# A post-norm decoder layer: cross attention's output kept as two halves, the routing arithmetic cut into single steps, and VectorE and TensorE held to the written order

## The chip, the cores and the metric

The kernel runs on one core of a Trainium2 chip. A core has a matrix engine (TensorE, PE in the profile, with its weight loads as PEld), a vector engine (VectorE, DVE), a scalar engine for activations (ScalarE, ACT), a general engine (GpSimd, POOL) and a synchronising engine (SyncE, SP) that mostly issues transfers. Each takes its instructions in order; they wait for each other by semaphores, and 16 DMA engines move data between the on-chip memory (SBUF), the accumulators (PSUM) and DRAM. The metric is the device time of one execution in microseconds, as the median of several runs. Everything is computed in fp32 precision.

## What is computed

The reference is one decoder layer on x of 16 batches of 100 tokens, 512 wide (1600 tokens), cut here to what matters:

```python
x = layernorm(x + self_attention(x))               # 16 heads of 32
x = layernorm(x + cross_attention(x, ctx))         # 16 query heads of 128, 4 key heads, 361 keys
x = layernorm(x + moe(x))                          # 8 experts, the best 2 for each token

def cross_attention(hidden, enc, mask):
    q = rmsnorm(hidden @ Wq + bq);  k = rmsnorm(enc @ Wk + bk);  v = enc @ Wv + bv
    probs = softmax(q @ k.T / sqrt(128) + mask)    # 4 query heads share a key head
    return (probs @ v) @ Wo

def moe(x):
    logits = x @ router_w + router_b
    vals, idx = top_k(logits, 2);  w = softmax(vals)
    h = silu(x @ expert_w[e] + expert_b[e])        # for the two experts of each token
    out = (sum of w * h) @ proj_w + proj_b
    y = x + out
    return norm_w * y / sqrt(mean(y * y) + 1e-6)
```

## The kernel before

**Pairs.** A product in fp32 precision is made of three products of rounded operands. `split` (L134) turns a tensor into a `Pair`: the high half is a copy rounded to fp32r (L139 on ScalarE, or L141 on VectorE), and the low half is what the rounding left, a subtraction (L142, on VectorE or GpSimd). `mm3` (L145) then issues high by high, high by low and low by high (L147 to L149), and `mmk` does so over the pieces of the contraction. So every operand of a product costs two element-wise passes ahead of it.

**Stages.** (a) Self attention by groups of four batches. (b) Its output product, the first layernorm, and the queries of cross attention, which are stored to DRAM (`qd`). (c) Cross attention, a loop over 64 steps (batch b, key head g), each with four heads. A step loads and splits its queries (`x_load`), makes scores (`x_scores`), exponentials and their scaling, transposes the probabilities and splits them (`x_turn`), and multiplies with the values (`x_attend`). When the third piece of keys is done, `x_attend` copies the accumulator `av` to a tile `o` on ScalarE (L839), adding the bias of the values, and stores it to `od` in DRAM (L844); there are two such tiles. During the same steps the keys and values of the next batch are projected. (d) The output product of cross attention: 13 tiles t of up to 128 tokens, each in four *parts* (t, g). `d_load` (L869) loads a part of `od`, splits it (high on ScalarE, low on GpSimd and VectorE in turn), `d_part` (L878) multiplies it: 12 products of 512 columns with 3 for each of the four heads, so 12 `mm3` products in all. `d_norm` (L898) adds the residual and does the second layernorm on VectorE, with two short activations on ScalarE in between; `d_turn` (L980) transposes the result, and `d_logits` (L997) makes the router's logits. The last three tiles (TAIL) are taken together, g outermost. (e) The experts: the tokens are sorted into 32 slots of 128 rows, each of one expert. `e_gather` fetches the rows of a slot by an indirect transfer from GpSimd's queue, `e_turn` transposes and splits them, `e_product` multiplies with the expert's weights, which are addressed by a register, and `e_out` adds the bias and applies Silu. (f) Gathering the two results of each token, the last product, and the two last norms.

**Routing.** `choose` (L1110) finds the two best experts of three tiles at a time, and each token's rank within its expert; `settle` (L1204) works out which slots are open, and `slots` (L1306) turns that into row indices by 36 or more tiny products. All of it is small VectorE arithmetic, 0.15 to 1.5 us each, in one long chain of dependences with a few products in it. It is done twice: for the first nine tiles, which give the first 11 slots, and for the rest.

**Order.** The program is written as a sequence, but the scheduler of the tile framework (`schedule_with_timeline_sim=True`) decides the order on each engine from its own model of durations; a dependence of the kind "no semaphore, order only" (`in_turn`, `tc.keep_in_program_order`) ties two instructions of an engine, and `tc.high_priority` moves a group ahead. In the kernel before, the routing functions are issued in one go at their place in the text, with high priority for the second round, and the weights of an expert are loaded by `load_expert` (L1389), four rows in one go. The parts that the scheduler put into the end of cross attention are products that fill PE's time between the dependent steps there.

Of the kernel before, what the change touches and what calls it, by code (L numbers as in the profile page):

```python
# [19 lines left out]
KC = D // 128  # L20
# [43 lines left out]
def tile_decoder_layer(  # L64
# [69 lines left out]

    def split(dst, src, high=None, low=None):

        high, low = high or nc.scalar, low or nc.vector
        if high is nc.scalar:
            ins = nc.scalar.copy(dst.h, src)  # L139
        else:  # L140
            ins = high.tensor_copy(dst.h, src)  # L141
        low.tensor_tensor(dst.l, src, dst.h.bitcast(FP), ALU.subtract)  # L142
        return ins
# [77 lines left out]
    od = [dram.tile([128, NH, 128], FP, name=f"od_{t}") for t in range(NT)]  # L221
# [601 lines left out]
    def x_attend(b, g, i):  # L823
# [14 lines left out]
        o = w2.tile([128, GR, S], FP, name=f"o2_{b}_{g}", tag="o")  # L838
        nc.scalar.activation(o, av, AF.Identity, bias=bvT[:, g : g + 1])  # L839
        a = 0  # L840
        while a < S:
            t, r = divmod(b * S + a, 128)
            m = min(S - a, 128 - r)
            nc.sync.dma_start(  # L844
                od[t][:, g * GR : (g + 1) * GR, r : r + m], o[:, :, a : a + m]
            )
            a += m
# [13 lines left out]
    def d_open():  # L861
        kv_l.close()
        inp["d"] = pool(d_i, "d_in", 2)
# [5 lines left out]
    def d_load(i):  # L869
        t, g = parts[i]  # L870
        n = TT[t][1]
        p = inp["d"]
        of = p.tile([128, GR, 128], FP, name=f"of_{t}_{g}", tag="of")
        nc.sync.dma_start(of[:, :, :n], od[t][:, g * GR : (g + 1) * GR, :n])
        OT[t, g] = pair(p, [128, GR, 128], f"ot_{t}_{g}", tag="ot")
        split(OT[t, g][:, :, :n], of[:, :, :n], low=nc.vector if i % 2 else nc.gpsimd)
# [20 lines left out]

    def d_norm(t):  # L898
        t0, n = TT[t]
        acc = X1.pop(t)  # L900
        p = w3 if t >= HEAD else inp["d"]
        x2 = p.tile([128, D], FP, name=f"x1_{t}", tag="x1", bufs=1 if t < HEAD else 3)
        nc.sync.dma_start(x2[:n], x1d[t][:n])
# [3 lines left out]
        X2[t] = x2  # L907
# [6 lines left out]
    for i, (b, g) in enumerate(order):  # L914
        if b == B - 1:
            if g == 0:
                d_open()
                d_load(0)
            for j in range(HEAD * g, HEAD * (g + 1)):
                d_load(j + 1)  # L920
                d_part(j)
                if parts[j][1] == NKV - 1:
# [36 lines left out]
    xsp = pool(fin, "k_x", 4, side="right")  # L959
    gs = ExitStack()  # L960
# [19 lines left out]
    def d_turn(t):  # L980
# [12 lines left out]
        nc.gpsimd.tensor_tensor(x2[:n], x2[:n], pb[:n], ALU.add)  # L993
# [115 lines left out]

    def choose(a, b):  # L1110
# [5 lines left out]
        for j in range(2):  # L1116

            nc.vector.tensor_reduce(top[:, j, a:b], vals, AX.X, ALU.max)
            hit = table("hit", sh)
            nc.vector.tensor_tensor(  # L1120
                hit, vals, top[:, j, a:b].unsqueeze(2).to_broadcast(sh), ALU.is_equal
            )
            nc.vector.tensor_tensor(hit, hit, num_b, ALU.mult)
            nc.vector.tensor_reduce(place[:, j, a:b], hit, AX.X, ALU.min)
            nc.vector.tensor_tensor(
# [4 lines left out]
            )  # L1130
            if j == 0:
# [3 lines left out]
                )  # L1135
                vals = rest
        if b == NT:

            nc.vector.memset(one[64:, :, NT - 1, :], 0.0)
        nc.vector.tensor_tensor(  # L1140
            chosen[:, a:b, :], one[:, 0, a:b, :], one[:, 1, a:b, :], ALU.add
        )
        for t in range(a, b):
            nc.vector.tensor_tensor(
                cum[:, t + 1, :], cum[:, t, :], chosen[:, t, :], ALU.add
            )
        o1, o2 = 2 * NE, (2 + m) * NE
# [21 lines left out]
        )  # L1169
        sh2 = [128, 2, m, NE]  # L1170
# [6 lines left out]
        )  # L1177
        rj = gw.tile([128, 2, m], FP, name=f"rj_{a}", tag=f"rj_{m}")
        nc.vector.tensor_reduce(rj, mine, AX.X, ALU.add)
        ri = gw.tile([128, 2, m], I32, name=f"ri_{a}", tag=f"ri_{m}")  # L1180
        nc.vector.tensor_copy(ri, rj)
        nc.vector.tensor_scalar(ri, ri, 127, None, ALU.bitwise_and)
        nc.vector.tensor_copy(lo[:, :, a:b], ri)

        nc.vector.tensor_scalar(rj, place[:, :, a:b], float(NE), None, ALU.add)
        nc.vector.scalar_tensor_tensor(
            opens[:, :, a:b], lo[:, :, a:b], 0.0, rj, ALU.is_equal, ALU.mult
        )
        if b == NT:
            nc.vector.memset(opens[64:, :, NT - 1 :], 0.0)  # L1190
            nc.vector.memset(token[64:, NT - 1 :], 0.0)

        for j in range(2):
            for t in range(a, b):
# [7 lines left out]
                )  # L1202

    def settle(a, b):  # L1204
# [5 lines left out]
        if a == 0:  # L1210
            by_128(full, count[:, m, :], "full")

        up = table("up", [128, m + 1, NE])
        nc.vector.tensor_scalar(up, count, 127.0, None, ALU.add)
        had = table("had", [128, m + 1, NE])
        by_128(had, up, f"had_{a}")

        opn = table("opn", sh)
        nc.vector.tensor_tensor(opn, had[:, 1:, :], had[:, :m, :], ALU.subtract)
        had = had[:, :m, :]  # L1220
        sh4 = [128, m, NE, NE]

        def before_it(these, here, less, name):
# [7 lines left out]
            )  # L1231
            new = table(name, sh)
            nc.vector.tensor_reduce(new, part, AX.X, ALU.add)
            nc.vector.tensor_reduce(here[:, a:b], these, AX.X, ALU.add)
            tri = parts_of([128, 1, m, b])[:, 0]
# [5 lines left out]
            )  # L1241
            till = table("till", [128, m])
            nc.vector.tensor_reduce(till, tri, AX.X, ALU.add)
            nc.vector.scalar_tensor_tensor(
# [6 lines left out]
            )  # L1251
            return new


        new = before_it(opn, opened, 0 if a else -EARLY, "new")
        if a == 0:
# [3 lines left out]
            )  # L1260
            nc.vector.tensor_tensor(fills, fills, opn, ALU.mult)
            first = before_it(fills, filled, 0, "first")
# [3 lines left out]
            )  # L1266

            nc.vector.scalar_tensor_tensor(
                fills, first, float(EARLY), fills, ALU.is_lt, ALU.mult
            )  # L1270
# [614 lines left out]
```

## Time and profile before

| | |
|---|---|
| median of 3 runs | 1400.51 us (1400.23 to 1403.87) |
| profiled execution, its own time | 1408.13 us |
| its span, first to last instruction | 1406.4 us |
| PE busy | 1331.6 us (95%) |
| VectorE busy | 942.8 us (67%) |
| ScalarE busy | 756.4 us (54%) |
| GpSimd busy | 710.3 us (51%) |
| mean granted clock of PE | 0.976 |

How to read it: the profile is one execution, 7.6 us longer than the median of the three timed runs, and 1.7 us of its time lie outside the span. A matmul's end is modelled, so a busy PE may hold slow products; the distance from one product's start to the next tells its pace. The stages lie about so: self attention to 200 us, stage (b) to 400, cross attention to 1074 with its first output parts from 993 on, the rest of the parts to about 1206, the experts to about 1365, the end to 1406.

### The profile page before, as it was taken

What the parts mean: (1) busy time and instruction counts of PE and PEld (TensorE: products, weight loads), DVE (VectorE), ACT (ScalarE), POOL (GpSimd) and SP (SyncE); (2) the same over time, 40 slices, a digit from 0 to 9 for tenths busy, and PEclk for the clock granted to TensorE, in tenths of its full rate; (3) what the DMA queues carried; (4) which work ended last, traced back from release to release, by engine and by line L of the source; (5) the groups of instructions that cost most, each with busy time, mean ns of one, the idle gap of its engine ahead of it and who ended that gap; (6) DMA issues with size and microseconds to landing.
All of it is one profiled execution on the core that took longest, in us unless ns stands there. A gap on an engine that the chain in (4) does not pass through costs nothing.

```text
span 1406.4 us, 25135 instructions
## 1 busy us (share of the span) xinstructions
PE 1331.6 (95%) x7928; PEld 1105.0 (79%) x7928; DVE 942.8 (67%) x2933; ACT 756.4 (54%) x1897; POOL 710.3 (51%) x840
## 2 busy tenths in 40 slices
PE   8999989999999999999999999999999898899894
PEld 7888868888778888888888888878887676677773
DVE  5776677776467777777777767767654558754576
ACT  4666643444446666666666666656654233333356
POOL 6878753344245555555555555545455444532530
PEclk9999989999999999999999999999999999899997
DMA  5221363544442122322233312322446545667883
GB/s 170 68 74 58 124 194 96 131 92 114 100 94 72 42 70 71 76 78 70 71 76 78 74 46 67 73 68 51 118 101 182 178 167 164 211 214 240 256 252 118
DMA packets 199160, 161.74 MB, mean 115 GB/s; under 512 B 133581, under 2 KB 153265, under 8 KB 199029
## 3 DMA queue, kind: packets, MB, share of 16 engines
q1 hardware_dynamic: 189191, 139.77, 36.2%
q0 software_dynamic: 4576, 14.95, 3.4%
q10 hardware_dynamic: 5262, 5.41, 1.3%
q8 instruction: 65, 1.06, 0.3%
q14 instruction: 66, 0.54, 0.1%
HBM read 107.25 MB, written 50.99 MB: 113 GB/s over the span
## 4 chain that ended last, share of the span: by engine, by line
PE 68%; DVE 14%; DMA 7%; ACT 4%; issue 3%; POOL 1%; SPq 1%; ACTq 1%; DVEq 0%; POOLq 0%
PE pq L147 4%; PE pq L148 4%; PE pq L149 4%; PE pv L147 4%; PE pv L148 4%; PE pv L149 4%; PE ptp L819 3%; PE pk L147 3%; PE pk L149 3%; PE pk L148 3%; PE s L147 3%; PE s L148 3%; PE s L149 3%; PE av L148 2%; PE av L147 2%
## 5 line engine op out<-in xcount | busy, mean ns | idle before, releaser
L811 POOL TENSOR_SCALAR p<-p,sums 100x361 f32<-100x361 f32 x256 | 146.4, 577 | 99.4 <-DVE sums L810 88.2
L798 DVE CUSTOM_DVE_ANT_0 p<-s,nmask 100x361 f32<-100x361 f32 x256 | 133.0, 527 | 63.4 <-PE s L149 54.7
L809 ACT ACTIVATE p<-p,nm 100x361 f32<-100x361 f32 x256 | 153.2, 601 | 39.6 <-DVE nm L798 36.3
L142 DVE TENSOR_TENSOR pT_l<-ptp,pT_h 128x400 fp32r<-128x400 f32 (+1 forms) x192 | 107.5, 568 | 57.2 <-ACT pT_h L139 56.8
L147 PE MATMUL pq<-WH 128*128 128x512 f32 (+2 forms) x272 | 107.2, 394 | 5.3 <-DVE WH L141 5.3
L819 PE MATMUL ptp<-ident,p 100*128 100x100 f32 (+1 forms) x768 | 107.4, 252 | 0.0
L139 ACT CAST pT_h<-ptp 128x400 fp32r<-128x400 f32 (+1 forms) x192 | 91.2, 487 | 30.1 <-PE ptp L819 29.7
L142 POOL TENSOR_TENSOR cT_l<-cf,cT_h 128x512 fp32r<-128x512 f32 (+1 forms) x48 | 54.4, 1133 | 103.4 <-ACT cT_h L139 101.5
L819 PEld LDWEIGHTS ptp<-ident,p 100*128 100x128 f32 (+1 forms) x768 | 95.4, 151 | 13.3 <-POOL p L811 2.3
L148 PE MATMUL pq<-WL,WH 128*128 128x512 f32 (+2 forms) x272 | 104.9, 385 | 0.0
L149 PE MATMUL pq<-WH,WL 128*128 128x512 f32 (+2 forms) x272 | 104.6, 385 | 0.0
L149 PE MATMUL acc<-WH,ot_l 128*128 128x512 f32 (+1 forms) x208 | 85.7, 413 | 7.3 <-DVE ot_l L142 5.8
L147 PE MATMUL acc<-WH,ot_h 128*128 128x512 f32 (+1 forms) x208 | 85.1, 409 | 5.0 <-ACT ot_h L139 5.0
L147 PE MATMUL s<-kT_h,WH 128*100 128x362 f32 x256 | 88.1, 355 | 0.7 <-ACT kT_h L139 0.7
L147 PE MATMUL av<-pT_h,WH 128*128 128x400 f32 (+1 forms) x192 | 76.8, 400 | 9.0 <-ACT pT_h L139 8.6
L666 POOL TENSOR_TENSOR qs<-qs,r_q 128x512 f32<-128x512 f32 (+1 forms) x52 | 54.0, 1068 | 60.9 <-DVE r_q L171 49.4
L149 PE MATMUL s<-kT_h,WL 128*100 128x362 f32 x256 | 84.3, 329 | 0.0
L148 PE MATMUL s<-kT_l,WH 128*100 128x362 f32 x256 | 83.7, 327 | 0.0
L148 PE MATMUL acc<-WL,ot_h 128*128 128x512 f32 (+1 forms) x208 | 83.6, 402 | 0.0
L142 POOL TENSOR_TENSOR WL<-qf,WH 128x400 fp32r<-128x400 f32 x64 | 67.3, 1052 | 30.5 <-ACT WH L139 26.9
L147 PE MATMUL pv<-WH,cT_h 128*128 128x512 f32 (+1 forms) x192 | 79.8, 416 | 0.9 <-DVE WL L142 0.9
L148 PE MATMUL pv<-WL,cT_h 128*128 128x512 f32 (+1 forms) x192 | 77.9, 406 | 0.0
(348 smaller groups left out, 3990.6 us busy)
## 6 DMA issues: line engine op xcount, KB each, us to landing
qf<-qd SPq DMA_DIRECT2D x64, 200.0 KB
of<-od SPq DMA_DIRECT2D x48, 256.0 KB
cf<-in_ctxT SPq DMA_DIRECT2D x16, 722.0 KB
eb<-in_expert_b SPq DMA_DIRECT2D x32, 256.0 KB
ysd<-h SPq DMA_DIRECT2D x32, 256.0 KB
f_e<-in_expert_w SPq DMA_DIRECT2D x30, 256.0 KB
f_wq<-in_Wq SPq DMA_DIRECT2D x16, 256.0 KB
f_wo<-in_Wo SPq DMA_DIRECT2D x16, 256.0 KB
```

The lines of the kernel that those rows point to most:

```text
L139: ins = nc.scalar.copy(dst.h, src)
L142: low.tensor_tensor(dst.l, src, dst.h.bitcast(FP), ALU.subtract)
L147: nc.tensor.matmul(out, a.h, b.h, start=start, stop=False)
L148: nc.tensor.matmul(out, a.h, b.l, start=False, stop=False)
L149: nc.tensor.matmul(out, a.l, b.h, start=False, stop=stop)
L666: nc.gpsimd.tensor_tensor(qr[:, hs, :], qr[:, hs, :], rs[:n, hs].unsqueeze(2).to_broadcast([n, GR, HD2]), ALU.mult,)
L798: nc.vector.tensor_tensor_reduce(out=p, in0=sc[:, :SE], in1=nmask, scale=1.0, scalar=BIG, op0=ALU.add, op1=ALU.min, accum_out=nm,)
L809: nc.scalar.activation(p, p, AF.Exp, bias=nm, scale=-1.0, accum_out=sh)
L811: nc.gpsimd.tensor_scalar(p, p, sh, 1.0, ALU.mult, ALU.mult)
L819: nc.tensor.transpose(pt[:n, h, :], probs[h][:, c0 : c0 + n], ident[:S, :S])
```

## The change

- *Halves in DRAM.* `od` holds, for each head, a high and a low half. At the end of a step `x_attend` makes the high half on ScalarE, as before but rounded, and the low half by one more VectorE instruction that reads `av` from PSUM, adds the bias and subtracts the high half. The tile `o` is twice as large, and there is one of it instead of two. Stores and loads of `od` carry twice the bytes, and `d_load` with its two splits is replaced by `d_fetch`, a transfer alone, which runs three parts ahead with four buffers.
- *Single steps.* `choose`, `settle` and `slots` are generators that yield after each VectorE instruction, and PAUSE ahead of the products that use what came before. `route(n)` issues the next n steps: 12 after each part, and 15, 14 and 11 between the expert products.
- *Program order.* `pin` ties all VectorE instructions, and all PE instructions, from part 12 (t = 3, g = 0) to the expert product in whose step the routing ends, each to the one before it in the text. ScalarE, GpSimd and SyncE are still ordered by the scheduler. With this the text itself is put in order: `d_turn(t - 1)` goes ahead of part g = 2 instead of g = 1, expert rows are split one at a time at given parts (`e_rows`), the residual is loaded ahead at g = 2 (`d_x1`), the first two slots are transposed ahead of the last two parts, the second round's products come after expert products 3 and 7 (counted from 0), gathers of slots are issued earlier, and the bias of the last three tiles (`d_bias`) after expert weights.
- *Gates.* The weights of the two experts were made by Exp, an addition, a reciprocal and a product; they are made by Tanh of half the difference of the logits and two affine instructions.

The diff, cut to its core:

```diff
-    od = [dram.tile([128, NH, 128], FP, name=f"od_{t}") for t in range(NT)]
+    od = [dram.tile([128, NH, 2, 128], FP, name=f"od_{t}") for t in range(NT)]
...
-        o = w2.tile([128, GR, S], FP, name=f"o2_{b}_{g}", tag="o")
-        nc.scalar.activation(o, av, AF.Identity, bias=bvT[:, g : g + 1])
+        o = w2.tile([128, GR, 2, S], FR, name=f"o2_{b}_{g}", tag="o", bufs=1)
+        bias = bvT[:, g : g + 1]
+        nc.scalar.activation(o[:, :, 0, :], av, AF.Identity, bias=bias)
+        nc.vector.scalar_tensor_tensor(
+            o[:, :, 1, :], av, bias, o[:, :, 0, :].bitcast(FP), ALU.add, ALU.subtract,
+        )
...
-    def d_load(i):
-        of = p.tile([128, GR, 128], FP, name=f"of_{t}_{g}", tag="of")
-        nc.sync.dma_start(of[:, :, :n], od[t][:, g * GR : (g + 1) * GR, :n])
-        OT[t, g] = pair(p, [128, GR, 128], f"ot_{t}_{g}", tag="ot")
-        split(OT[t, g][:, :, :n], of[:, :, :n], low=nc.vector if i % 2 else nc.gpsimd)
+    def d_fetch(upto):
+        for i in range(fetched[0], min(upto, len(parts))):
+            p = inp["d2" if i > HEAD * NKV and i % 4 == 2 else "d"]
+            o = p.tile([128, GR, 2, 128], FR, name=f"ot_{t}_{g}", tag="ot")
+            nc.sync.dma_start(o[:, :, :, :n].bitcast(FP), od[t][:, g * GR : (g + 1) * GR, :, :n])
+            OT[t, g] = Pair(o[:, :, 0, :], o[:, :, 1, :])
...
+    def route(n):
+        while n and routing:
+            what = next(routing[0], None)
+            if what is None and routing[0].gi_frame is None:
+                routing.pop(0)
+                continue
+            if what == PAUSE:
+                return
+            n -= 1
+
+    def pin(engine, since):
+        prev = None
+        for ins in nc.cur_bb.bb.instructions[since:]:
+            if ins.engine == engine:
+                if prev is not None:
+                    tc.add_manual_dep(ins, prev.name, ...NoSync..., reason="pin")
+                prev = ins
...
+    PINNED = 3 * NKV
     for i in range(HEAD * NKV, len(parts)):
         t, g = parts[i]
-        if i + 1 < len(parts):
-            d_load(i + 1)
+        d_fetch(i + 4)
+        if g == 2:
+            d_x1(t)
+        e_rows(i)
         among = {}
         if t < NT - TAIL:
-            if g == 1:
+            if g == 2:
                 d_turn(t - 1)
...
         elif (t, g) == (NT - 1, NKV - 1):
             d_turn(NT - TAIL)
+            e_turn(1)
+        elif (t, g) == (NT - 2, NKV - 1):
+            e_turn(0)
         d_part(i, among)
...
         if t % 3 == 0 and t <= CUT and g == 3:
-            choose(t - 3, t)
+            routing.append(choose(t - 3, t))
+        if (t, g) == (CUT, 3):
+            routing += [settle(0, CUT), slots(0, EARLY, CUT)]
         if (t, g) == (NT - 1, 0):
-            choose(CUT, CUT + 1)
-        if (t, g) == (CUT, 3):
-            settle(0, CUT)
-            slots(0, EARLY, CUT)
-        if (t, g) == (NT - 1, 1):
+            routing.append(choose(CUT, CUT + 1))
+        if i == PINNED:
+            since = traced()
+        if i < len(parts) - TAIL:
+            route(12)
+        if i == len(parts) - TAIL - 1:
             for k in range(4):
                 e_gather(k)
...
+    at_once(NT - TAIL)
+    d_turn(NT - 2)
+    load_last(wo_slot[3])
+    at_once(NT - 2)
+    d_norm(NT - 1)
+    e_product(0)
     e_turn(2)
+    e_gather(4)
+    d_turn(NT - 1)
...
+    e_out(0)
     e_product(1, {1: lambda: at_once(NT - 1)})
     e_turn(3)
+    e_gather(5)
+    e_out(1)
+    routing += [choose(CUT + 1, NT), settle(CUT, NT), slots(EARLY, NSL, NT)]
+    route(15)
+    e_product(2)
+    e_out(2)
+    route(14)
...
-    nc.scalar.activation(ex, ex, AF.Exp)
+        nc.scalar.activation(th, th, AF.Tanh, scale=0.5)
...
         if TAIL <= i < NSL:
             e_product(i)
             e_out(i)
+            if routing:
+                route(11)
+                if not routing:
+                    slot, g1, g2 = gates()
+                    for e in (nc.vector.engine, nc.tensor.engine):
+                        pin(e, since)
+            while len(SLOT) > asked[0] < min(i + 5, NSL):
+                e_gather(asked[0])
+                asked[0] += 1
```

## The prediction

> **What bounds the kernel now.** I read the page's busy shares and slices first, then what PE waits for, then a table by stretches of 25 us, then the timelines of PE, VectorE and GpSimd around the worst stretches. PE is the bound:
>
> ```profile
> PE 1331.6 (95%) x7928; PEld 1105.0 (79%) x7928; DVE 942.8 (67%) x2933; ACT 756.4 (54%) x1897; POOL 710.3 (51%) x840
> ...
> PE   8999989999999999999999999999999898899894
> PEclk9999989999999999999999999999999999899997
> ```
>
> The change moves no product off PE, so time can come only from PE's gaps: 75 us (span less busy), and what slow products hide. In the waits of PE, named by what ended them, these belong to the change:
>
> ```profile
> PE av L147 <- ACT pT_h L139: 8.6, 10, 2.6
> PE acc L149 <- DVE ot_l L142: 5.8, 4, 3.6
> PE acc L147 <- ACT ot_h L139: 5.0, 2, 3.7
> PE av L148 <- DVE pT_l L142: 3.8, 19, 0.3
> PE acc L149 <- POOL ot_l L142: 1.4, 2, 1.3
> ```
>
> 12.2 us (5.8 + 5.0 + 1.4) are waits for the halves of cross attention's output; 12.4 us are cross attention's own waits for its probabilities. The stretches (us; busy of PE, PEld, DVE, ACT, POOL, granted clock, DMA share, GB/s) show where PE loses:
>
> ```profile
> 600.00:625.00 25.00, 24.70 (x141) 20.76 (x140) 19.40 (x74) 17.09 (x48) 13.70 (x18) 1.00 0.31 83
> 1100.00:1125.00 25.00, 19.64 (x93) 15.19 (x91) 13.97 (x38) 6.90 (x14) 11.38 (x9) 0.93 0.57 185
> 1175.00:1200.00 25.00, 20.28 (x107) 14.25 (x108) 24.17 (x50) 8.74 (x16) 15.25 (x13) 0.86 0.50 153
> 1200.00:1225.00 25.00, 21.62 (x109) 16.44 (x108) 19.28 (x63) 9.31 (x20) 14.25 (x13) 0.87 0.66 206
> 1250.00:1275.00 25.00, 22.47 (x125) 17.45 (x124) 8.40 (x15) 6.80 (x12) 8.59 (x9) 0.86 0.67 214
> ```
>
> Cross attention is dense with VectorE at about 75%. In the parts and experts PE idles 2.5 to 5.4 us a stretch, and at 1175 VectorE has nothing left. A gap also costs afterwards: after the 3.60 us one, products follow at 0.43 us, where 0.23 is normal (1097.72, 1097.95, 1098.18):
>
> ```profile
> 1182.45 0.69 PE L149 MATMUL acc<-WH,ot_l 128*64 128x512 f32 x1 [3.60 <-DVE ot_l L142]
> 1182.94 0.63 PE L147 MATMUL acc<-WH,ot_h 128*64 128x512 f32 x1
> 1183.37 0.63 PE L148 MATMUL acc<-WL,ot_h 128*64 128x512 f32 x1
> ```
>
> The clock's record shows half clock in pieces of 3.4 or 6.8 us, so such a gap costs 1.7 or 3.4 us more. Last, VectorE's and GpSimd's timelines in the routing:
>
> ```profile
> 1171.28 0.16 DVE L1093 CAST i_full<-gb 128x8 int32<-128x8 f32 x1
> ...
> 1172.12 1.29 DVE L1094 TENSOR_SCALAR i_full<-i_full 128x8 int32<-128x8 int32 x1
> ```
>
> ```profile
> 1170.83 3.82 POOL L142 TENSOR_TENSOR WL<-f_e,WH 128x512 fp32r<-128x512 f32 x3
> 1174.62 1.29 POOL L142 TENSOR_TENSOR ot_l<-of,ot_h 128x512 fp32r<-128x512 f32 x1
> ```
>
> While GpSimd runs a subtraction, about one tiny VectorE instruction takes 1.1 to 1.3 us instead of 0.2.
>
> **The change, part by part.** The sum is made against the profiled execution, 1408.1 us (1406.4 span and 1.7 around it); it is 7.6 above the median 1400.5, and I take the difference over to the median unchanged.
>
> *Waits for halves, removed: -17.3.* The 12.2 us go, because a part needs only a transfer now. With them goes half clock after the gaps near 1108 (3.4 us) and 1182 (6.8 us): half of 10.2, 5.1 us. The 52 removed splits also free ScalarE (0.6 us each), VectorE (26 x 0.7) and GpSimd (26 x 1.2); none of it is on the path beyond these waits.
>
> *What is late next: the first routing, +6.0.* The gap at 1182 covered part of the routing's chain. In the changed order PE has, between the products of `choose(6, 9)` and the 36 of `slots`, five parts: 5 x 12 x 0.23 = 13.8, with logits 14.3 us. VectorE has, before those 36 are free: 0.6 to see the first product, 2.8 for the rest of `choose`, and `settle`. From 1171.28 to 1198.66 before (27.4 us) I take off 2.5 for splits of `ot`, 2.8 for `choose`, and 12.2 of lengthening, which leaves about 10. GpSimd ran 14 instructions in that time, 0.87 us of lengthening each; now its halves of `ot` are gone and five expert rows and a bias are left, 6 x 0.87 = 5.2. Sum 18.6 against 14.3: PE, in order, waits 4.3 us, and 1.7 at half clock. Behind the waiting product stand parts 47 to 51, which the old order could have run; that is the price of the fixed order. The Trainium skill's page "SBUF — State Buffer", section "Who interferes with whom", speaks against it: a VectorE instruction with two SBUF inputs, or in a two-port mode, is fully blocked for the whole of a GpSimd instruction that reads SBUF. By the rule six instructions of 1.27 us lengthen the chain by 7.6 instead of 5.2, and this item is 8.4 instead of 6.0. I keep the row.
>
> *Start of the expert products: +0.6.* Before, 1200 to 1225 had 3.4 us idle, and 10.2 us of half clock followed: 8.5 in all. Now `d_turn(10)` is one part (2.8) and one transpose (0.5) behind a norm that takes 4.1 (from 1161.45 to 1165.44, and the wait for the product): about 1; logits right behind a transpose wait for ScalarE's copy: 1; the first product waits for the last rows' low halves on VectorE: 2; `d_turn(12)` for its norm: 1.7; half clock 3.4. Sum 9.1. The earlier `ptx` waits (1.4) go, `d_turn(9)` gains as much.
>
> *Second routing: -4.4.* 1250 to 1275 lost 2.5 idle and 3.4 at half clock, from the gather of the first late slot. Now the second `slots` come after product 7, with two products and two transposes (6.5 us) before the first late slot is transposed, against 5.7 us of transfer and some issue time: about 1 left, and 0.5 for VectorE, which has 11 steps (2.4 us), a bias and a split (1.4) for each 3.3 us of PE.
>
> *Cross attention: +3.* 64 more VectorE instructions, none like them in the trace; the nearest row is the low half of the probabilities, same shape and also from PSUM, 568 ns: 36 us of VectorE, from 75% to 81%. Below: nothing, as VectorE's idle covers it, and slightly less, since the order shifts. Above: all of it, 36. PE waited 29 times for these probabilities, and half an instruction more on some of them is 3. The store waits behind it on SP, with query loads queued after; nothing reads it for many steps. The single `o` adds a wait on ScalarE: 0.6 + 0.6 + issue 0.9 + landing 2.6 to 4.3 (stores of `xbd` and `ysd` in the chain) is 4.7 to 6.4, and copies to `o` came no closer than 6.4 us where I looked (609.13, 615.53). Covered, barely; probabilities stand behind it on ScalarE. The stores are 57344 more packets of 400 bytes or less (112 x 512). At the 43 ns mean of the queue (36.2% of 16 x 1406 us over 189191) they take 154 us of all 16 engines over 630 us, the share from 0.28 to 0.53. The skill's "DMA: Bandwidth & Descriptors", "Specifications", calls pieces under 512 bytes read-modify-write; at twice the time, share 0.77, landing would pass 6.4 and this item would be rival two. I keep the row, since pieces this short already are most packets.
>
> *Fewer parts inside cross attention's end: +2.* 10 instead of 17 parts fill PE there, so VectorE and ScalarE are closer to the limit; 0 to 8.
>
> *Transfers of the parts: +1.* At full pace a tile takes 12 us and moves 3.3 MB (2 MB halves, rows, residual, stores), 277 GB/s; the trace holds 255 to 269 at its end. Three parts of lead are 8.3 us. 0 to 8.
>
> *Tanh: 0.* Two table loads of 1.28 us leave ScalarE at 1224 and 1231, where it is 38% busy (9.51 of 25); without that slack they are worth 2.6.
>
> Sum: -17.3 + 6.0 + 0.6 - 4.4 + 3 + 2 + 1 = -9.1: 1399 for the profiled execution, **1391** as median.
>
> **Rivals.** *One, the written order fits:* the chain is met, products start without gaps, cross attention hides its instruction: -17.3 - 5.9 + 1.5 + 2 = -20, with 4 of the start's half clock -24: 1377. For it: VectorE loses 18 us of splits exactly where it was full. Against: the chain still needs more than PE's five parts. *Two, slower: cross attention pays.* VectorE's new instruction and ScalarE's wait for the only `o` delay probabilities in each step. At 0.4 us a step, 64 x 0.4 = 26 in place of the 3: 1414. It decides from (9.1 + 3 + 4.2) / 64 = 0.25 us a step. For it: PE there waits for just these two engines; against: 25% of VectorE is idle. *Three, waits are only exchanged:* routing at its upper end (8.4) and the start of the products at twice its 5.7 us of waits: -9.1 + 2.4 + 5.7 = -1, 1400.
>
> **How the numbers follow.** 0.3%, 4.2 us, is about what a measurement of this kernel can tell from no change. My forecast has 0.45 (its own range 1382 to 1401), rival one 0.2, two 0.2, three 0.15. Faster: 0.34 + 0.2 + 0.05 = 0.59; the same: 0.09 + 0.07 = 0.16; slower: 0.02 + 0.2 + 0.03 = 0.25. The range goes to rival one and past it by some of the bounds, and to rival two: 1371 to 1414.
>
> **What would show it.** Right: no wait of `acc` but for transfers; one gap of about 4 us ahead of the `slots` products; cross attention's waits for `pT_h` and `pT_l` up by 3 us; `pte` waiting about 1 us for the first late gather. Wrong: ScalarE waiting for `od` stores, cross attention ending well after 1058 (1074 less the 19 us of the seven parts it no longer holds, plus 3), or `acc` waiting for DMA.

## The result: 0.6% slower, where 0.65% faster was forecast

The changed kernel took 1409.5 us (median of 8 runs, 1406.4 to 1411.2); the kernel before took 1400.4 on the same chip. The ratio is 1.0057 (95% interval 1.004 to 1.0075). The forecast was 1391: the time lies inside the range (1371 to 1414), but on the other side of no change. The profiled execution took 1408.3 us, span 1406.6. The page's busy times, and two rows of its slices:

```profile
PE 1323.1 (94%) x7928; PEld 1103.2 (78%) x7928; DVE 957.1 (68%) x2970; ACT 726.3 (52%) x1843; POOL 678.4 (48%) x814
...
PE   8999979999999999999999999999987997889995
PEclk9999989999999999999999999999988998899997
```

ScalarE and GpSimd lost 30 us of work each and TensorE is still the bound; its new dip (8, 7 in slices 30 and 31) is where cross attention ends, at 1042. What TensorE waits for in the changed kernel, in us, times and the longest one:

```profile
PE gb L1433 <- DVE is_in L1416: 9.5, 2, 8.8
PE acc L149 <- DMA ot<-od: 8.4, 4, 5.8
PE ptx L1008 <- DVE x L185: 6.5, 3, 3.0
PE av L150 <- DVE pT_l L144: 5.5, 22, 0.5
...
PE av L149 <- ACT pT_h L141: 3.1, 9, 0.5
```

The 12.2 us for `ot_h` and `ot_l` are gone, and cross attention's waits for probabilities have fallen from 12.4 to 8.6 instead of rising by 3. Against that stand 9.5 us ahead of `slots`, 8.4 for transfers of parts and 6.5 for norms. The stretches, with the columns of the table before:

```profile
1025.00:1050.00 25.00, 18.35 (x98) 15.26 (x97) 9.48 (x29) 9.52 (x24) 5.58 (x8) 0.87 0.66 180
1100.00:1125.00 25.00, 25.00 (x122) 20.54 (x121) 5.84 (x19) 4.37 (x10) 7.65 (x6) 1.00 0.76 256
1175.00:1200.00 25.00, 15.50 (x89) 11.10 (x88) 18.00 (x52) 4.34 (x7) 11.10 (x10) 0.80 0.59 188
1200.00:1225.00 25.00, 19.60 (x85) 14.63 (x84) 17.02 (x42) 6.32 (x15) 10.18 (x9) 0.80 0.49 144
```

1100 to 1125, which had lost 5.4 us to the halves, is full, at full clock and with 256 GB/s of transfers. The routing at 1175 lost 4.7 us before and loses 9.5 now. In terms of stages: the first `acc`, the first product of the output parts, came at 993.2 us before and comes at 979.5 now (13.7 us earlier); from there to the end it was 413.2 us and is 427.1. Before, and now:

```profile
993.22 0.40 PE L147 MATMUL acc<-WH,ot_h 128*128 128x512 f32 x1
```

```profile
979.48 0.50 PE L149 MATMUL acc<-WH,ot 128*128 128x512 f32 x1
```

These two traces have the same span, since the one of before is 7.7 us above its kernel's median and the one of now 1.2 below: the two differences cancel (-13.7 and +13.9) where the medians say +9.1, so each is known to some 9 us only. Three things need a cause: what was won in cross attention, where +3 was forecast; what the halves brought; and what was lost after 979.

### The profile page after: what moved, and what is told of

Same layout as the page of the kernel before. It is cut to its first block, busy times and chain, and to the rows that moved or that the text cites. A ratio compares the mean times of both kernels' runs of the same rounds, so it can differ in the third digit from the quotient of the medians.

```text
span 1406.6 us, 25107 instructions
## 1 busy us (share of the span) xinstructions
PE 1323.1 (94%) x7928; PEld 1103.2 (78%) x7928; DVE 957.1 (68%) x2970; ACT 726.3 (52%) x1843; POOL 678.4 (48%) x814
## 3 DMA queue, kind: packets, MB, share of 16 engines
q1 hardware_dynamic: 248583, 165.99, 42.4%
## 5 line engine op out<-in xcount | busy, mean ns | idle before, releaser
L149 PE MATMUL acc<-WH,ot 128*128 128x512 f32 (+1 forms) x208 | 90.0, 433 | 8.4 <-DMA ot<-od 8.4
L150 PE MATMUL acc<-WL,ot 128*128 128x512 f32 (+1 forms) x208 | 85.1, 409 | 0.0
L151 PE MATMUL acc<-WH,ot 128*128 128x512 f32 (+1 forms) x208 | 84.9, 408 | 0.0
L149 PE MATMUL pk<-WH,cT_h 128*128 128x512 f32 (+1 forms) x192 | 76.8, 400 | 0.0
```

Of the source, the lines that this page charges most:

```text
L149: nc.tensor.matmul(out, a.h, b.h, start=start, stop=False)
L150: nc.tensor.matmul(out, a.h, b.l, start=False, stop=False)
L151: nc.tensor.matmul(out, a.l, b.h, start=False, stop=stop)
```

## The experiments

Each number is a ratio to the kernel before on the same chip, with its 95% interval. The level of the kernel before itself differed between chips (1400 to 1418 us), so kernels timed on one chip compare most firmly: e1, e2, e3 and e6 on one; e7, e9, e10 and e11 on a second; e13, e15, e16 and e17 on a third; e18, e19, e20 and c1 on a fourth; e22 and e23 on a fifth. A trace is one execution; waits and starts are read from it.

**The halves alone (e1).** The kernel before, with only this part of the diff (three buffers for parts):

```diff
-        d_load(i + 1)
+        d_fetch(i + 3)
...
```

> The kernel before with the halves in DRAM alone (stores and loads of pairs, one tile o, three buffers for parts); order, routing and gates as before. Theory A (what the halves save is real, and the changed kernel loses it again in its written order and its buffers): the 12.2 us of waits for ot_h and ot_l go, cross attention pays at most 3: 1386 to 1396, against 1400.4 before. Rival R (cross attention pays for the VectorE instruction, the single o and the longer stores): 1405 to 1414, with PE waiting more than 12 us for the probabilities.

Measured: 1383.7 us, ratio 0.9825 (0.98 to 0.9849), better than theory A expected. Rival R is out. First `acc` at 979.0, as in the changed kernel, and 400.0 us from there to the end. So the rest of the change, measured against this kernel, costs 2.4% (1.0057 / 0.9825). In e1, too, TensorE waits 7.2 us ahead of `slots` (0.3 before): with the halves gone from the path this chain is the next late thing, in the scheduler's order as well.

**Where cross attention's gain comes from (e7, e13, e18).** First the VectorE instruction and the single `o`, in the kernel before:

```diff
-        o = w2.tile([128, GR, S], FP, name=f"o2_{b}_{g}", tag="o")
+        o = w2.tile([128, GR, S], FP, name=f"o2_{b}_{g}", tag="o", bufs=1)
...
+        more = w2.tile([128, GR, S], FR, name=f"more_{b}_{g}", tag="more", bufs=1)
+        nc.vector.scalar_tensor_tensor(more, av, bias, o, ALU.add, ALU.subtract)
```

> The kernel before with one thing of the change: in each step of cross attention the VectorE instruction that reads av and o (its result goes to a tile that nothing reads), and a single tile o; od, its stores, loads and splits as before. In the two kernels with halves cross attention reached its first acc 14 us earlier than before although it held 64 more VectorE instructions, and TensorE's products stood in another order there (a scheduler decides). Theory O (the order on TensorE decides, the instruction and the single o cost next to nothing): this kernel has a third order, so its first acc lies within 6 us of either 979 or 993, and the rest is as before: ratio 0.99 to 1.003. Rival R (the instruction costs at least 0.25 us a step, and only the missing splits and lighter stores of the halves hide it): first acc after 1005, ratio 1.01 or more.

Measured: 1.0052 (1.0038 to 1.0067), first `acc` at 1009.5, in a trace that is 7 us above its median. Too slow for O; R had the first `acc` right (after 1005) and the ratio too high (1.01). The instruction and the single `o` were thus not free in this order; TensorE's waits for `pT_h` rose from 8.6 to 14.5 us. Next, TensorE's order of the kernel with halves, imposed on the kernel before:

```diff
+    for this, prev in zip(ranks[1:], ranks):
+        tc.add_manual_dep(products[this], products[prev].name, ...NoSync..., reason="order")
```

> The kernel before, with nothing of the change, but TensorE's products inside cross attention held to the order that they have in the kernel with halves alone (which is that of the changed kernel too), up to the first acc. Theory O (cross attention got faster by that order, not by the halves or in spite of the VectorE instruction): first acc at 977 to 984 instead of 993, the longest wait for pT_h below 1 us instead of 2.6, ratio 0.988 to 0.995. Rival H (the halves themselves or the lighter end of the step gave it): first acc at 990 or later, ratio 0.998 to 1.003.

Measured: 1.0098 (1.007 to 1.0126), first `acc` at 1015.3. Theory O fell: that order alone makes it worse, beyond what rival H had too. What e7 and e13 share with the kernel before, and the faster kernels lack, was found in ScalarE's waits. Before, changed, and with halves alone:

```profile
ACT WH L139 <- DMA f_wo<-in_Wo: 25.3, 16, 3.3
```

```profile
ACT WH L141 <- DMA f_wo<-in_Wo: 0.7, 2, 0.5
```

```profile
ACT WH L139 <- DMA f_wo<-in_Wo: 0.8, 1, 0.8
```

In e7 it was 30.5 us and in e13 30.0. `f_wo` are the 16 rows of the output weights that are loaded and split during cross attention. The timelines of ScalarE and then of PE in the kernel before show what stood behind one of these waits:

```profile
930.62 0.62 ACT L139 CAST WH<-f_wo 128x512 fp32r<-128x512 f32 x1 [3.31 <-DMA f_wo<-in_Wo]
931.14 0.48 ACT L139 CAST pT_h<-ptp 105x400 fp32r<-105x400 f32 x1
```

```profile
931.68 0.70 PE L147 MATMUL av<-pT_h,WH 105*128 105x400 f32 x1 [2.62 <-ACT pT_h L139]
932.29 0.70 PE L148 MATMUL av<-pT_l,WH 105*128 105x400 f32 x1
```

The row's split waits 3.31 us for its transfer, the probabilities stand behind it in ScalarE's order, and TensorE waits 2.62 us and then runs slow products (0.61 us from one start to the next; the granted clock of 800 to 975 us was 0.97 in the kernel before and 1.00 in the changed kernel, e1 and e18). With the halves the scheduler happened to put the splits where their rows had landed. One tie in the kernel before does that alone:

```diff
-            load_row(f"wo_{w}", wo_slot[w], Wo4[w], k)
+            fetch_row(f"wo_{w}", wo_slot[w], Wo4[w], k)
+            in_turn(split_row(f"wo_{w}", k), high_last[0])
...
```

> The kernel before with one tie on ScalarE: the high half of each of the 16 weight rows f_wo stands behind pT_h of the third piece of keys, not ahead of it. Theory F (cross attention got faster because ScalarE no longer waits for a transfer ahead of probabilities; the halves are not what did it): ScalarE's waits for f_wo fall from 25.3 us to below 5, PE's for pT_h from 8.6 to about 4, first acc at 979 to 986, ratio 0.990 to 0.996. Rival H (the halves' lighter end or other orders gave it): first acc at 990 or later, ratio 0.998 or more.

Measured: 1390.4 us, 0.9914 (0.9894 to 0.9933). ScalarE's waits for `f_wo`:

```profile
ACT WH L139 <- DMA f_wo<-in_Wo: 5.9, 4, 1.7
```

TensorE's for `pT_h` fell to 1.3 us, and the first `acc` came at 981.2:

```profile
981.21 0.40 PE L147 MATMUL acc<-WH,ot_h 128*128 128x512 f32 x1
```

Theory F holds: some 12 us (0.0086 of the time) were lost to a wait at the head of ScalarE's queue, with the probabilities standing behind it, and the change removed this by accident. That it is worth as much inside the changed kernel follows from its own waits for `f_wo` (0.7 us); putting the splits back in front there was not tried.

**The fixed order (e2, c1, e10, e11, e15, e16).** The changed kernel without `pin`:

```diff
-                    for e in (nc.vector.engine, nc.tensor.engine):
-                        pin(e, since)
```

> The changed kernel without the dependences that hold VectorE and PE to the written order; the text keeps its order, the scheduler may move things again. Theory B (the written order puts the products of slots 3 parts too early): the wait of 8.8 us ahead of them goes below 4 and with it some of the half clock: 1396 to 1403 against 1409.5. Theory C (the fourth buffer for parts comes free only with cross attention's memory): the wait of 5.8 us for ot at cross attention's end stays, since this is ahead of the pinned stretch or at its start. Rival R: no change, 1409.

Measured: 1392.1 us, 0.9873 (0.9852 to 0.9894). The wait ahead of `slots` fell to 1.5 us, as theory B had it, but the gain is at least twice B's; a wait of 6.2 us for `ot` stayed, as theory C had it. Its largest waits on PE:

```profile
PE pte L1478 <- DMA xs<-x2d,idx: 11.9, 4, 5.1
PE acc L149 <- DMA ot<-od: 10.0, 4, 6.2
```

Here the first products of `slots` stand after 51.4 parts, in the changed kernel after 47, and TensorE waits for the gathers instead. Waits for VectorE in 1040 to 1300 us sum to 8.5 us, against 26.9 in the changed kernel. The changed kernel itself was run once more beside later ones:

> The changed kernel itself, beside the others on the same chip: 1.004 to 1.008, as before; its waits on PE for VectorE after cross attention about 27 us, for transfers about 8.

Measured: 1411.4 us, 1.0056 (1.0038 to 1.0074). So the fixed order costs 1.0056 - 0.9873 = 0.018, 26 us, as the sum of all that it does. Which engine's order? Only TensorE's, then only VectorE's (`for e in (nc.tensor.engine,)`, `for e in (nc.vector.engine,)`):

> The changed kernel with only TensorE held to the written order, VectorE free. Theory P (TensorE's order costs: it stands in front of the products of slots, of transposes and of the second routing while parts and products behind them could run): waits as with both held, ratio 1.002 to 1.008. Rival V (VectorE's order costs: its chain is held up behind norms, biases and h): the wait ahead of slots falls below 4 us and the ratio to 0.985 to 0.992.

> The changed kernel with only VectorE held to the written order, TensorE free. Theory P: the scheduler puts the first products of slots after part 52 instead of 47, the wait ahead of them is below 4 us, ratio 0.985 to 0.992, as with neither held. Rival V: no better than with both held, 1.002 to 1.008.

Measured: TensorE held 0.9926 (0.9898 to 0.9955), VectorE held 1.0047 (1.0026 to 1.0069). Theory P fell: TensorE's order alone costs 0.005, VectorE's alone 0.017; with TensorE held, freeing VectorE gives 0.013. With TensorE held and VectorE free the wait ahead of `slots` stayed (10.5 us), so that rival V was nearly right about the time (0.985 to 0.992) and wrong about that wait. In which stretch? Both engines held to the last part only, and held only from there on:

> The changed kernel with VectorE and TensorE held to the written order from part 12 to the last part only, free in the experts. The fixed order costs 0.018 of the time in all, and nearly all of that through VectorE. If it is lost in the parts (the first routing's chain and the norms that stand in one row there), this is 1.000 to 1.006; if in the experts (the second routing between products), 0.987 to 0.992. By the waits of the trace two thirds lie in the parts: 0.999.

> The changed kernel with both engines held to the written order only from the end of the parts to the expert product in whose step the routing ends. If the fixed order is lost in the parts, this is 0.987 to 0.991 as with no fixed order; if in the experts, 1.000 or more. By the waits of the trace one third: 0.993.

Measured: parts 1.0021 (1.0007 to 1.0034), experts 0.9905 (0.9883 to 0.9927). Against 0.9873 that is 0.015 in the parts and 0.003 in the experts. VectorE's waits in 1040 to 1300 us say what it does there. Changed kernel, then without `pin`:

```profile
DVE lg L1044 <- PE gb L1040: 52.5, 10, 8.9
```

```profile
DVE lg L1044 <- PE gb L1040: 11.0, 9, 3.3
```

In the written order VectorE stands 52.5 us ahead of the small addition that takes up a tile's logits, and norms and routing queue behind it. The first step of `choose(6, 9)`, in the changed kernel and then without `pin`:

```profile
1163.58 0.17 DVE L1188 TENSOR_REDUCE top<-lg 128x3 f32<-128x24 f32 x1
```

```profile
1154.71 0.18 DVE L1188 TENSOR_REDUCE top<-lg 128x3 f32<-128x24 f32 x1
```

It comes 8.9 us later. With TensorE free and VectorE held (e11) the timeline of VectorE shows the reason best:

```profile
1154.81 0.17 DVE L1044 TENSOR_TENSOR lg<-gb,rb 128x8 f32<-128x8 f32 x1 [11.18 <-PE gb L1040]
1154.92 0.69 DVE L926 TENSOR_TENSOR x<-acc,x 128x512 f32<-128x512 f32 x1
...
1167.54 0.17 DVE L1044 TENSOR_TENSOR lg<-gb,rb 128x8 f32<-128x8 f32 x1 [9.11 <-PE gb L1040]
1167.65 0.69 DVE L926 TENSOR_TENSOR x<-acc,x 128x512 f32<-128x512 f32 x1
...
1171.08 0.17 DVE L1188 TENSOR_REDUCE top<-lg 128x3 f32<-128x24 f32 x1
```

Twice it idles 9 to 11 us; then a norm of 3.4 us comes ahead of `choose(6, 9)`, whose first step is the last row. TensorE's last part began its last product 20 us after that step; the chain took about 32, and TensorE waited 10.9.

**What in VectorE's order (e19, e23).** Both engines held, but one kind of VectorE instruction left out of the order: the routing, or the norms.

```diff
-            if ins.engine == engine:
+            if ins.engine == engine and not (
+                engine == nc.vector.engine and ins.name in free
+            ):
...
```

> The changed kernel with both engines held to the written order, but the routing's VectorE instructions left out of it (norms, logits, splits and h stay in order among themselves; TensorE is held in full). Theory V1 (the routing in one row with norms and logits is what the fixed VectorE order costs): as with VectorE free, 0.991 to 0.996. Rival V2 (the order of the rest, norms ahead of splits, biases and h, costs): 1.002 to 1.006, as with both held.

> The changed kernel with TensorE held to the written order and VectorE too, except that the norms are left out of VectorE's order. Theory V3 (norms, which wait for the end of a tile's parts, stand ahead of logits and routing, and routing ahead of norms: each alone gives a part): 0.996 to 1.002. Rival V4 (the rest, splits and h, costs what the routing does not): 1.004 to 1.007.

Measured: routing free 1.0008 (0.9994 to 1.0022), norms free 0.9999 (0.9983 to 1.0015); all of VectorE free was 0.9926. Each gives 0.005 to 0.006 of 0.013. V1 hoped for too much; V3 holds: each gives a part. Both freed together were not run, so whether the two add up, and what is left for the splits, biases and `h` that stayed in order, is open.

**Moving the products of `slots` (e3).** Two more pauses ahead of them, and the first two slots transposed after the last part:

```diff
         yield PAUSE
+        if a == 0:
+            yield PAUSE
+            yield PAUSE
...
```

> The changed kernel with the products of slots two parts later (after part 48 instead of 46, counted from 0), and the transposes of the first two slots after the last part. Theory B: the wait of PE ahead of those products falls by two parts, 8.8 to about 3.2 us, with less half clock after it: 1400 to 1405 against 1409.5, if the gathers do not become late in turn (pte would wait). Theory C: the wait of 5.8 us for ot at cross attention's end is as it was. Rival R: 1409.

Measured: 1413.4 us, ratio 1.001 (0.9994 to 1.0027). In microseconds the kernel missed its figure, since the chip was slower; as a ratio it is 0.5% below the changed kernel, as theory B expected. The wait was 5.5 us instead of 8.8, not 3.2.

**The fourth buffer (e6, e9, e17).** After 1041.84, when cross attention ends, TensorE waits 5.75 us for a part, and the next products start 0.43 us apart instead of 0.23:

```profile
1041.84 0.35 PE L151 MATMUL av<-pT_h,WL 105*128 105x400 f32 x1
1047.93 0.80 PE L149 MATMUL acc<-WH,ot 128*128 128x512 f32 x1 [5.75 <-DMA ot<-od]
1048.53 0.63 PE L150 MATMUL acc<-WL,ot 128*128 128x512 f32 x1
1048.95 0.63 PE L151 MATMUL acc<-WH,ot 128*128 128x512 f32 x1
```

The load was issued after that end, at 1043.19 (SyncE's queue):

```profile
1041.10 1.99 SPq L529 DMA_DIRECT2D f_e<-in_expert_w  x1
1043.19 0.38 SPq L890 DMA_DIRECT2D ot<-od  x1
```

It is part (1, 2). In `d_fetch` every part with `i % 4 == 2` uses the pool `d2`, which is opened behind cross attention and gets memory that is free only when cross attention's last product has run. So tiles 1, 2 and 3 each stop at g = 2, and 4 + 2 + 2 + 2 = 10 parts fit into cross attention's end. The edit:

```diff
-            p = inp["d2" if i > HEAD * NKV and i % 4 == 2 else "d"]
+            p = inp["d2" if i > 4 * NKV and i % 4 == 2 else "d"]
```

> The changed kernel with the fourth buffer for parts used only from part 17 on, so that no part inside cross attention needs memory that comes free at its end. Theory C: 14 parts instead of 10 can lie inside cross attention, the waits of acc for ot of 5.8 and 2.2 us and about 10 us recorded at half clock after them go: 1396 to 1402 against 1409.5; cross attention's last product comes about 11 us later, the last acc about 8 to 12 earlier. If instead the expert rows and the od stores ahead of the loads in SP's queue make the wait, it stays above 4 us and the time at 1409.

Measured: 1.0048 (1.0028 to 1.0069), not told apart from the changed kernel. As theory C had it, 14 parts lie inside cross attention instead of 10 and the wait for `ot` went, so that the rows and stores ahead in SyncE's queue did not make it; the time that C promised did not come, for another wait took its place:

```profile
1061.68 2.23 PE L1008 MATMUL ptx<-ident,x 128*128 128x128 f32 x8 [10.55 <-DVE x L185]
```

The transposes of the normalised tiles stand next in TensorE's written order. Their norms need the residual, whose tiles (`x1` in the pool `w3`) also lie in memory that cross attention frees. The same edit without the fixed order:

> The changed kernel without the fixed order and with the fourth buffer used only from part 17 on. With the order fixed, the second edit alone took the waits for ot away and put one of 10.6 us for the norm of tile 0 in their place, since the next transposes stand ahead of the parts in the text. Theory C2 (a wait taken away comes back only because the order is fixed): here TensorE may run parts in that time, the waits of 6.2 and 2.8 us for ot after cross attention go and nothing comes in their place: ratio 0.980 to 0.983, against 0.987 without this edit. Rival: a norm or the residual's tile (its memory too comes free with cross attention) is the next wait, of over 5 us: 0.986 to 0.988.

Measured: 0.982 (0.9794 to 0.9847) against 0.9873: 7 us, the time that C2 had. TensorE ran parts while the residual came. It was not free of exchange: the waits ahead of `slots` rose from 1.5 to 9.7 us. With TensorE held from part 20 on, VectorE free, `slots` later and this edit (e17):

> The changed kernel with only TensorE held to the written order, and from part 20 on instead of 12, the products of slots two parts later, and the fourth buffer used from part 17 on. With TensorE alone held the ratio was 0.9926, with waits of 10.5 us ahead of slots and 8.5 us for ot. Theory V (a free VectorE lets both edits keep what they take away): 5.6 and 8 us less and some half clock: 0.978 to 0.983. Rival (each wait comes back at the next thing that is late, a norm or a gather): 0.988 to 0.993.

Measured: 0.9949 (0.9929 to 0.9969): slower than even the rival had it, and no better than TensorE held alone (0.9926). Waits of 6.2 us for `chosen` and 5.4 for a norm took the place of those removed.

**GpSimd beside the chain, and norms inside it (e20, e22).** In e9, the low halves of the last 14 expert rows on VectorE instead of GpSimd:

```diff
+                split(units[f"e_{e}"][:, k], row, nc.scalar, nc.vector)
...
```

> The kernel without fixed order and with the fourth buffer late (0.982), and with the low halves of the last 14 expert rows made by VectorE instead of GpSimd. Theory G (GpSimd's subtractions lengthen the routing's chain by about 1 us each where VectorE would need 0.67 for the same work): the chain from choose(6, 9) to is_in, 39 us with 12 to 14 of them beside it, is 3 to 5 us shorter, the waits for is_in (6.5 and 3.2) fall by as much, ratio 0.977 to 0.980. Rival (VectorE is short of time there, and 14 more instructions of 0.67 us, 9.4 us, cost more than the lengthening): 0.983 to 0.987.

Measured: 0.9873 (0.9851 to 0.9894), the rival at its upper end, and 0.005 slower than e9: the waits ahead of `slots` were 10.3 us instead of 9.7. In the kernel with halves alone, the last norms behind the routing (`in_turn(ins, settled[0])` on the norm's first instruction):

> The kernel with halves alone, and on VectorE the norms of the last three tiles tied behind the second is_in of the first routing. In the trace without the tie 1.4 us of norms and a row's high half lie in the chain's last 6 us. Theory N (they delay is_in): waits ahead of slots fall from 7.2 us to 4 or 5 and the norms, now later, are covered by the first gathers' transfer: ratio 0.978 to 0.981. Rival (the norms become the next wait: ptx for x, before logits of the last tiles): 0.983 to 0.987.

Measured: 0.9846 (0.9821 to 0.9871), not told apart from e1. The first wait ahead of `slots` went; waits for gathers rose from 6.3 to 9.2 us, and one of 4.4 for a norm came.

## Why the prediction was wrong, point by point

The step that failed is the price of the fixed order. The prediction put it at one wait of TensorE ahead of the products of `slots` (4.3 us, and 1.7 at half clock), added +0.6 and -4.4 for what the new order does later, and gave VectorE's standing in its own written order no term. The runs show 26 us for it (e2), with VectorE's order as the larger part (0.013 to 0.017 of 0.018). The 12 us that came by luck in cross attention kept the time inside the range.

- **Waits for halves, -17.3, with cross attention's own +3: right in sum.** e18 takes away the accident on ScalarE, and from there (0.9914) to the halves alone (0.9825) it is 0.009, 12.5 us, known to about 4, against 14.3 forecast. In the traces it lies behind the first `acc`: 407.5 us to the end in e18, 400.0 in e1. The +3 does not show: the kernel with halves reaches its first `acc` 2 us ahead of e18. In the kernel before it is not free (e7, 1.0052), but there the waits for `f_wo` grew with it, so its own cost stays open. Of the stores, the feared share of 0.53 was 0.37 in 400 to 1000 us (0.29 before): by the queue's shares (42.4% of 16 x 1406.6 us over 248583 packets, less 36.2% over 189191) an added packet took 23.5 ns, not 43. The rule of the Trainium skill that I had set beside the row ("DMA: Bandwidth & Descriptors", "Specifications": pieces under 512 bytes are read-modify-write), priced at twice the time, was further off; no run here shows such a price. ScalarE did wait for the stores of the single `o`, and TensorE's waits for probabilities fell all the same:

```profile
ACT o L842 <- DMA od<-o: 5.4, 4, 2.2
```

  Rival two is out by e1's ratio.
- **Missed altogether: -12 in cross attention.** The list of PE's waits showed `pT_h` on ScalarE, 8.6 us, and I counted it as cross attention's own. ScalarE's waits, which I did not show, named `f_wo`. So the kernel before held a gain that had nothing to do with the change.
- **First routing, +6.0: mis-sized.** The wait was 9.5 us instead of 4.3, and the granted clock was 0.50 in the 10 us from 1187, of which 6 lie behind the wait's end at 1190.81: about 3 us more, where 1.7 was forecast.

```profile
1187.00:1197.00 10.00, 5.46 (x46) 4.46 (x46) 6.69 (x28) 0.00 (x0) 3.06 (x3) 0.50 0.23 63
```

  The chain, from the last `cum` (its end at 1166.7), which the products of `choose` read, to the second `is_in` (1191.7), took 24.9 us instead of 18.6. In that time GpSimd ran 9 instructions, not 6, and the VectorE instructions that they lengthened took 7.5 us more than their usual time: 0.83 each. The trace's row (0.87) was right and its count wrong; blocked for the whole of each, as the prediction read the Trainium skill's "SBUF — State Buffer", "Who interferes with whom", they would have taken 9 x 1.27 = 11.4 more, by estimate; the page gives the shared ports to whoever issues first, so that this is the most it allows. In the changed kernel, two such rows of VectorE and an undisturbed one, and GpSimd's beside them:

```profile
1182.16 1.20 DVE L1367 SCALAR_TENSOR_TENSOR new<-first,new 128x72 f32<-128x72 f32 x1
1183.28 1.31 DVE L1372 SCALAR_TENSOR_TENSOR fills<-first,fills 128x72 f32<-128x72 f32 x1
1184.63 0.23 DVE L1376 TENSOR_TENSOR first<-first,new 128x72 f32<-128x72 f32 x1
```

```profile
1182.00 2.50 POOL L144 TENSOR_TENSOR WL<-f_e,WH 128x512 fp32r<-128x512 f32 x2 [0.52 <-ACT WH L141]
```

  The other 4 us are the forecast's arithmetic: I had taken 12.2 us of lengthening off the chain of before, and left 10 for `settle` where 13.8 was right.
- **The fixed order as a whole: 26 us.** I priced TensorE standing in front of `slots`, and followed no other queue. VectorE's 52.5 us of standing ahead of logits are not one wait but a lateness of what follows: TensorE's waits for VectorE between 1040 and 1300 us are 26.9 us, and 8.5 without the fixed order.
- **Second routing, -4.4, and start of the products, +0.6.** The start is near the forecast: 1200 to 1225 us idled 5.4 us, where its waits were put at 5.7. The gather of the first late slot did stop being waited for. But from 1225 to 1300 us the changed kernel waits 1.8 us for `rank` and 2.9 for `xsT_l`, where e2, in the scheduler's order, waits 5.0 for the gather: one was exchanged for the other. Holding the experts alone (e16) is 0.003 above e2, and the intervals overlap.
- **Fewer parts +2, transfers +1: mis-sized, and the cause was another.** Together 7 us (e9 against e2). It was not bandwidth (e6 moves the same bytes without that wait) but the memory of a fourth buffer. "10 instead of 17" was in the order of instructions; I did not ask why.
- **Tanh, 0.** Two table loads did go; the change was not tried alone.

Sum in ratios: the rows of `f_wo` -0.009 (before to e18), the halves -0.009 (to e1), then to e9, which adds the steps, the text's order and Tanh, -0.0005, buffers +0.005 (to e2), the fixed order +0.018 (to the changed kernel): +0.006. This is one chain of runs, so it must close and proves nothing by closing; a piece may be worth less in other company, as the buffers were (0.001 in the fixed order). Of the signs that the prediction named for being right, `acc` did wait for transfers alone, but the gap ahead of `slots` was 9.5 us and not 4, and the waits for probabilities fell. Of those for being wrong, `acc` waiting for DMA came true, ScalarE waiting for stores too but at no cost seen, and cross attention ended at 1042, before 1058 and not after. Two kernels beat both: halves alone (0.9825), and the changed kernel without the fixed order and with the fourth buffer late (0.982); they are not told apart.

## What to carry to other kernels

When an order is written out by hand, follow every engine's queue, not only the bound one's: here VectorE, standing before a small addition, delayed all that was written behind it. A wait on the bound engine that names another engine is half a reading; ask what that engine itself was waiting for, since it may be a transfer that has nothing to do with the product. Taking one wait away paid here only where something else might run: the same edit of the buffers gave nothing in a fixed order and 7 us in a free one.

## What was not expected of the hardware

Nothing of the chip itself, but two sizes: 57344 more short stores in cross attention raised the DMA share by 0.08 while TensorE's waits there did not grow; and a GpSimd subtraction of 1.27 us beside tiny VectorE instructions cost these 0.83 us on average, yet moving such subtractions to VectorE at 0.69 us each was 0.005 slower (e20).
